# A mixture-of-experts stage with side work: the order of calls on every engine, and side work in fixed steps

## The chip, the cores and the metric

The kernel runs on one core of a Trainium2 chip. The metric is device time in microseconds (us), the median of several runs. Names of engines: PE is TensorE's matmul, PEld its weight load, DVE is VectorE, ACT is ScalarE, POOL is GpSimd, SP is SyncE, which here only issues transfers.

## The reference, cut to what matters

Two blocks of cross attention and feed-forward follow one another on x of shape (4, 512, 512), fp32, so there are 2048 tokens of width 512:

```
x = x + tanh(g) * L0_xattn(layernorm(x), ctx)      # int8 codes, 16 heads
x = x + tanh(g) * L0_ffn(layernorm(x))             # 8 experts, top 2, and a shared expert
x = x + tanh(g) * L1_xattn(layernorm(x), ctx)      # fp8 codes, self and cross attention
x = x + tanh(g) * L1_ffn(x)                        # ternary weights
```

The second line is the mixture of experts. A token goes to two experts; each expert computes `silu(x w1) * (x w3) @ w2` with 448 hidden units. The fourth line's weights are made ternary: each of its two weight matrices is scaled by the mean of its absolute values, rounded and limited to -1, 0 and 1. That mean and these codes do not depend on x.

## The kernel before

**The stages.** `xattn_int8` is the first line, `moe` the second, `attend_and_feed` the third and fourth. Nearly the whole kernel is bound by TensorE. While the mixture of experts runs, the kernel also prepares weights for what follows. There are two kinds of this side work:

- *Split pieces.* `split_weights` makes 80 steps (class `Split`). Each loads a piece of 128 x 512 fp32 (`s_raw`, 256 KB), on VectorE scales and centres it (`centre`; pieces of the projection have nothing to centre), casts it to a high part on ScalarE and subtracts for the low part on GpSimd (`cut`, `s_hl`), and stores both parts (512 KB). The pool has two buffers each for `s_raw` and `s_hl`.
- *Block 4.* `Ffn.weights` makes a list of 26 steps for the ternary weights: 12 sums of absolute values of 128 x 1408 pieces (704 KB each, line 2287), two steps that turn sums into a scale (from line 2295), and 12 codings (the piece loaded again, three VectorE instructions, lines 2310 to 2312, and a store of 176 KB at 2313). They use four buffers in turn (`t_raw`).

**The mixture of experts.** Tokens are sorted by expert into 39 slots of 128 rows through `slots_in`, by indirect transfers. Before the slots, a written-out plan (`Beat`) runs the shared expert: `m_up` products and then 16 `m_po` products, and with them scales and scatters the rows of the slots and prepares 23 split pieces. The plan's last tick is 40; the last split piece is loaded in tick 36, cut in tick 38 and stored in tick 39.

Then comes the loop over slots. TensorE's order in slot s is: the up products of slot s+1 (`up`, 16 weight loads and matmuls into `pu` and `pw`), the transposes of slot s's hidden units (`turn_hidden`) and of slot s+2's rows (`turn_in`), and the down products of slot s-1 (`down`, into `po`). Each matmul in the program is two in the profile. SyncE loads the expert's w13 (two halves, line 1204) for slot s+3, into the buffer that `up(s+1)` gives back, and its w2 (line 1226) for slot s+1. There are two buffers of each, and a load is skipped where the slot two before had the same expert; the owner of the slot is read into registers first (`load`, line 1197). ScalarE issues the loads of rows (1208) and the stores of the results (1267).

**What sets the order.** Each engine runs its instructions in the order in which they stand in its queue. A wrapper, `Ordered`, makes the framework keep the order of the calls on one engine. Calls that don't go through it are placed by the framework's own scheduler, which may put them ahead of calls that stand before them in the text. In the slots of the kernel before only TensorE's calls go through `Ordered`; those of the other engines, the split pieces and block 4's steps do not. Line 245 is the wrapper's line, so every ordered instruction has L245 in the profile, and evacuations by `k.evac`, which takes VectorE and ScalarE in turn, have L110 and L112.

The last part of a slot's body, before:

```
            for _ in range(-(-len(split) // max(1, SLOTS - 5 - s))):
                split.pop(0)(ps)
            if ternary:
                ternary.pop(0)()
```

With 57 pieces left this is two a slot in slots 0 to 22 and one in slots 23 to 33. `split.pop(0)(ps)` loads, centres, cuts and stores in one call.

Of the kernel before, what the change touches and what calls it, by code (L numbers as in the profile page):

```python
# [11 lines left out]
F32 = mybir.dt.float32  # L12
# [5 lines left out]
AF = mybir.ActivationFunctionType  # L18
ALU = mybir.AluOpType
# [889 lines left out]
def moe(k, split, codes8, router, scratch, ffn):  # L909
# [13 lines left out]
    with ExitStack() as ctx:  # L923
# [270 lines left out]
        def load(s):  # L1194


            e = got["e", s] = nc.values_load(
                owners[:, s : s + 1], engines=(mybir.EngineType.SP,), min_val=0, max_val=E - 1,
                skip_runtime_bounds_check_because="it is at most E - 1 by construction",
            )  # L1200
            got["new", s] = None if s < 2 else e != got["e", s - 2]
            for c in (0, KC // 2):
                some = slice(c, c + KC // 2)
                nc.sync.dma_start(w13[s % 2][:, some], a["w13"][e][:, some], cond=got["new", s])

        def load_rows(s):
            work = p6.tile([P, 4, D], F32, tag="m_big", name=f"m_work{s}")
            rows = nc.scalar.dma_start(work[:, 0, :], rows_in[ts(s, P), :])
            for scatter in scatters:
                tc.add_manual_dep(  # L1210
                    rows.ins, scatter.name,
                    mybir.DependencyInfo(mybir.DependencyClass.Sync, mybir.DependencyReason.DATA),
                    reason="any of them may write a row of the slot",
                )

            tc.add_manual_dep(
                rows.ins, silus[-1].name,
                mybir.DependencyInfo(
                    mybir.DependencyClass.NoSync, mybir.DependencyReason.SCHED_ONLY
                ),  # L1220
                reason="order of ScalarE's queue",
            )
            got["work", s] = work

        def load_down(s):
            nc.sync.dma_start(w2[s % 2], a["w2"][got["e", s]], cond=got["new", s])

        PE = Ordered(tc, nc.tensor)

        def turn_in(s):  # L1230
            work = got["work", s]
            pt = ps_m.tile([P, KC, P], F32, tag="ps_m")
            for c in range(KC):
                PE.transpose(pt[:, c, :], work[:, 0, ts(c, P)], k.ident)
            k.evac(work[:, 1, :].rearrange("p (c t) -> p c t", c=KC), pt)

        def up(s):
            work, w = got["work", s], w13[s % 2]
            pu = ps_h.tile([P, HID], F32, tag="ps_h")
            pw = ps_h.tile([P, HID], F32, tag="ps_h")  # L1240
            for c in range(KC):
                for half, pp in enumerate((pu, pw)):
                    PE.matmul(
                        pp, lhsT=work[:, 1, ts(c, P)], rhs=w[:, c, half, :],
                        start=(c == 0), stop=(c == KC - 1),
                    )
            nc.scalar.activation(work[:, 2, 0:HID], pu, AF.Silu)
            nc.vector.tensor_tensor(work[:, 2, 0:HID], work[:, 2, 0:HID], pw, ALU.mult)  # L1248

        def turn_hidden(s):  # L1250
            work = got["work", s]
            pt = ps_m.tile([P, NHC, P], F32, tag="ps_m")
            for m in range(NHC):
                PE.transpose(pt[:HC, m, :], work[:, 2, ts(m, HC)], k.ident)
            k.evac(work[:HC, 3, :].rearrange("p (c t) -> p c t", c=NHC), pt[:HC])

        def down(s):
            work, w = got.pop(("work", s)), w2[s % 2]
            po = ps_o.tile([P, D], F32, tag="ps_o")
            for m in range(NHC):  # L1260
                PE.matmul(
                    po, lhsT=work[:HC, 3, ts(m, P)], rhs=w[:, m, :],
                    start=(m == 0), stop=(m == NHC - 1),
                )
            y = p4.tile([P, D], F32, tag="m_row", name=f"m_y{s}")
            nc.scalar.activation(y, po, AF.Copy, scale=k.tg[:, 2:3])
            nc.scalar.dma_start(rows_out[ts(s, P), :], y)

        ctxT, ws = [], {}

# [7 lines left out]
                ctxT[b], a["ctxT"][:, ts(b, S)].rearrange("(c p) t -> p c t", p=P)  # L1278
            )

        ternary = ffn.weights(codes8, ps_o)
        for s in range(4):
            load_rows(s)
        for s in range(2):
# [3 lines left out]
        up(0)  # L1288
        load(2)
        turn_in(1)  # L1290
        for s in range(SLOTS):

            if s + 1 < SLOTS:
                up(s + 1)
            if s + 3 < SLOTS:
                load(s + 3)
            turn_hidden(s)
            if s + 2 < SLOTS:
                turn_in(s + 2)
            if s:  # L1300
                down(s - 1)
                if s + 1 < SLOTS:
                    load_down(s + 1)
            if s + 4 < SLOTS:
                load_rows(s + 4)
            for _ in range(-(-len(split) // max(1, SLOTS - 5 - s))):
                split.pop(0)(ps)
            if ternary:
                ternary.pop(0)()
            if s == SLOTS - 4:  # L1310
                load_weights(0)
                load_context(0)
            elif s == SLOTS - 2:
                for c in range(KC):
                    centred(k, ws[0][:, c, 0:256], 2, nc.vector)
# [181 lines left out]
def split_weights(k):  # L1497
# [15 lines left out]
    class Split:  # L1513
# [23 lines left out]

        def store(self, SY):
            SY.dma_start(self.to, self.hl.bitcast(F32))

        def __call__(self, pool):
            self.load(pool, nc.sync)
            self.centre(nc.vector)
            self.cut(nc.scalar, nc.gpsimd)
            self.store(nc.sync)

    steps = []
    for i in range(NP):
# [680 lines left out]
class Ffn:  # L2229
# [32 lines left out]
        nc.sync.dma_start(self.mid[b * TB + t], k.x[:, t, :])  # L2262
        nc.sync.dma_start(k.x[:, t, :], self.mid[(b + 1) * TB + t])

    def weights(self, codes8, psum):


        k, nc, a = self.k, self.k.nc, self.k.a
        of = []
        for name, n, cols in (("w_gu", KC, 2 * F), ("w_dn", NF, D)):  # L2270
            flat = a[name].rearrange("p n o -> p (n o)")
            of.append((name, [flat[:, ts(i, F)] for i in range(n * cols // F)]))
        turn, got = [0], {}

        def piece(src):
            w = codes8.pool.tile(
                [P, 2048], F32, tag=f"g_xq{turn[0] % 4}", name=f"t_raw{turn[0]}"
            )
            turn[0] += 1
            nc.sync.dma_start(w[:, 0:F], src)  # L2280
            return w

        def add(name, i, n, src):
            if i == 0:
                got["part", name] = k.const.tile([P, n], F32, name=f"part_{name}")
            w = piece(src)
            nc.vector.tensor_reduce(
                got["part", name][:, i : i + 1], w[:, 0:F], AX.X, ALU.add,
                apply_absolute_value=True,
            )  # L2290

        def scale(name, n, inv):
            part = got["part", name]
            tot = k.small.tile([P, 1], F32, tag="t_tot")
            nc.vector.tensor_reduce(tot, part, AX.X, ALU.add)
            pm = psum.tile([P, 1], F32, tag="ps_o", name="t_pm")
            nc.tensor.matmul(pm, lhsT=k.ones, rhs=tot, start=True, stop=True)
            mean = k.small.tile([P, 1], F32, tag="t_mean")
            nc.vector.tensor_scalar(mean, pm, 1.0 / (P * n * F), 1e-5, ALU.mult, ALU.max)
            got["sc", name] = sc = k.const.tile([P, 1], F32, name=f"sc_{name}")  # L2300
            nc.vector.reciprocal(sc, mean)
            nc.vector.reciprocal(inv, sc)
            if name == "w_dn":
                nc.vector.tensor_tensor(inv, inv, k.tg[:, 3:4], ALU.mult)

        def code(name, src, lo):
            w = piece(src)
            sc = got["sc", name]
            raw, c8 = w[:, 0:F], w[:, F : F + F // 4].bitcast(F8)
            nc.vector.tensor_scalar(raw, raw, sc, 1.0, ALU.mult, ALU.min)  # L2310
            nc.vector.tensor_scalar(raw, raw, -1.0, MAGIC, ALU.max, ALU.add)
            nc.vector.tensor_scalar(c8, raw, -MAGIC, None, ALU.add, saturate=False)
            nc.sync.dma_start(self.codes[:, lo : lo + F], c8)

        steps, lo = [], 0
        for name, pieces in of:
            steps += [partial(add, name, i, len(pieces), p) for i, p in enumerate(pieces)]
        for (name, pieces), inv in zip(of, (self.inv_g, self.inv_dg)):
            steps.append(partial(scale, name, len(pieces), inv))
        for name, pieces in of:  # L2320
            for p in pieces:
                steps.append(partial(code, name, p, lo))
                lo += F
        return steps

# [98 lines left out]
```

## Time and profile before

| | |
|---|---|
| median of 3 runs | 3391.55 us (3390.26 to 3392.24) |
| profiled execution, its own time | 3394.43 us |
| its span | 3392.6 us |
| mean granted clock of TensorE | 0.985 |
| busy in the span: PE, DVE, ACT, POOL | 95%, 63%, 46%, 41% |
| the shared expert's products, `m_up` and `m_po` | 491 to 690 us |
| the slots, first `pu` to last `po` | 694 to 1138 us |
| issues of w13 halves and w2 | 117, of which most are skipped |

Times inside the profile are counted from the span's start. A line of a timeline gives the start, the duration, the engine, the line of the kernel, the operation, output<-input, and in brackets how long the engine sat idle before it and what ended that. A line of the waits gives who waited for whom, the total in us, the number of times and the longest.

### The profile page before, as it was taken

What the parts mean: (1) busy time and instruction counts of PE and PEld (TensorE: products, weight loads), DVE (VectorE), ACT (ScalarE), POOL (GpSimd) and SP (SyncE); (2) the same over time, 40 slices, a digit from 0 to 9 for tenths busy, and PEclk for the clock granted to TensorE, in tenths of its full rate; (3) what the DMA queues carried; (4) which work ended last, traced back from release to release, by engine and by line L of the source; (5) the groups of instructions that cost most, each with busy time, mean ns of one, the idle gap of its engine ahead of it and who ended that gap; (6) DMA issues with size and microseconds to landing.
All of it is one profiled execution on the core that took longest, in us unless ns stands there. A gap on an engine that the chain in (4) does not pass through costs nothing.

```text
span 3392.6 us, 47675 instructions
## 1 busy us (share of the span) xinstructions
PE 3218.7 (95%) x15466; PEld 2141.9 (63%) x15488; DVE 2144.5 (63%) x4551; ACT 1572.0 (46%) x4524; POOL 1377.5 (41%) x1568
## 2 busy tenths in 40 slices
PE   7999899899889999899999999999999999999997
PEld 4555554345445444577777777767777767777775
DVE  6888886443262455355587676687666786766567
ACT  4676661122222233455554555545545545555543
POOL 2001013412221255244466544566544575545443
PEclk9999999999899999999999999999999999999998
DMA  5544325845765444522232423323333322333210
GB/s 164 156 123 122 75 71 176 308 157 183 256 229 196 171 149 156 171 99 94 100 112 81 135 97 121 100 87 112 116 112 103 103 100 95 108 118 106 90 67 23
DMA packets 222008, 436.15 MB, mean 129 GB/s; under 512 B 23616, under 2 KB 82496, under 8 KB 220096
## 3 DMA queue, kind: packets, MB, share of 16 engines
q1 hardware_dynamic: 205408, 395.87, 35.6%
q10 hardware_dynamic: 11232, 20.45, 1.8%
q0 software_dynamic: 5120, 16.78, 1.5%
q8 instruction: 125, 2.05, 0.2%
q14 instruction: 123, 1.01, 0.1%
HBM read 387.33 MB, written 100.20 MB: 144 GB/s over the span
## 4 chain that ended last, share of the span: by engine, by line
PE 48%; DVE 8%; POOL 1%; ACT 1%; issue 1%; DVEq 0%; POOLq 0%; ACTq 0%
PE ps_w L245 11%; PE pss L245 10%; PE ps_p L245 10%; PE ps_o L245 9%; PE ps_t L245 8%; DVE f_y L245 2%; DVE nm L245 1%; DVE t_work L245 1%; DVE g_hn L245 1%; DVE f_e L245 1%; DVE g_pT L245 1%; POOL g_rstd L245 1%; DVE t_sm L245 1%; ACT junk L245 0%; DVE f_c L245 0%
## 5 line engine op out<-in xcount | busy, mean ns | idle before, releaser
L245 DVE TENSOR_REDUCE nm<-pss 128x1 f32<-128x512 f32 x768 | 523.6, 685 | 120.8 <-PE pss L245 116.2
L245 PEld LDWEIGHTS ps_w<-g_pT,g_v 128*128 128x128 f32 x2048 | 387.5, 190 | 299.5 <-issue 223.7
L245 ACT ACTIVATE g_p<-pss,nm 128x512 f32<-128x512 f32 x512 | 350.6, 685 | 479.3 <-DVE nm L245 439.2
L245 PE MATMUL ps_w<-g_pT,g_v 128*128 128x256 f32 x2048 | 528.5, 381 | 24.3 <-DVE f_y L245 13.6
L245 PE MATMUL pss<-g_kT,g_qT 128*128 128x512 f32 x1024 | 524.1, 594 | 0.9 <-ACT g_p L245 0.9
L245 POOL TENSOR_SCALAR g_p<-g_p,rs 128x512 f32<-128x512 f32 x512 | 366.8, 717 | 382.3 <-DVE rs L245 373.9
L245 PE MATMUL ps_t<-ident,g_p 128*128 128x128 f32 x2048 | 307.5, 273 | 0.0
L245 POOL TENSOR_TENSOR g_rstd<-ss,neghalf 128x4 f32<-128x4 f32 (+1 forms) x192 | 184.9, 963 | 298.5 <-ACT ss L245 298.5
L245 PE MATMUL ps_p<-g_wq,g_xq 128*128 128x512 f32 x1024 | 281.5, 416 | 5.6 <-DMA g_wq<-s_q 5.1
L245 PE MATMUL ps_o<-g_wp,g_cq 128*128 128x512 f32 x1024 | 286.1, 422 | 0.0
L245 DVE COPY g_pT<-ps_t 128x512 f32<-128x512 f32 x244 | 167.0, 684 | 166.6 <-PE ps_t L245 166.2
L245 POOL TENSOR_TENSOR f_t<-f_y,f_c 128x512 f32<-128x512 bf16 (+1 forms) x180 | 206.2, 1146 | 155.0 <-DVE f_c L245 87.2
L245 ACT COPY g_pT<-ps_t 128x512 f32<-128x512 f32 x268 | 155.9, 582 | 232.6 <-PE ps_t L245 232.6
L245 PEld LDWEIGHTS ps_t<-ident,g_p 128*128 128x128 f32 x2048 | 243.7, 141 | 26.3 <-POOL g_p L245 1.1
L245 ACT ACTIVATE p<-pss,nm 128x512 f32<-128x512 f32 x256 | 177.2, 693 | 134.0 <-DVE nm L245 127.8
L245 PE MATMUL m_pk<-m_wx,m_ctxT 128*128 128x512 f32 x512 | 230.0, 592 | 0.0
L245 PEld LDWEIGHTS ps_o<-g_wp,g_cq 128*128 128x128 f32 x1024 | 196.2, 192 | 41.3
L245 PEld LDWEIGHTS ps_p<-g_wq,g_xq 128*128 128x128 f32 x1024 | 190.9, 190 | 49.2 <-issue 6.8
L1536 POOL TENSOR_TENSOR s_hl<-s_raw,s_hl 128x512 fp32r<-128x512 f32 x57 | 76.4, 1350 | 341.8 <-ACT s_hl L1535 320.7
L245 DVE RECIPROCAL rs<-g_sm 128x1 f32<-128x1 f32 x512 | 82.5, 161 | 202.2 <-ACT g_p L245 200.3
L245 ACT ACTIVATE junk<-ps_p 128x128 f32<-128x128 f32 x640 | 176.7, 276 | 67.1 <-PE ps_p L245 52.9
L1248 DVE TENSOR_TENSOR m_work<-m_work,pw 128x448 f32<-128x448 f32 x39 | 24.2, 620 | 256.9 <-PE pw L245 220.5
(339 smaller groups left out, 5913.1 us busy)
## 6 DMA issues: line engine op xcount, KB each, us to landing
m_w<-in_w_dram SPq DMA_DIRECT2D x117, 896.0 KB
g_wp<-s_proj SPq DMA_DIRECT2D x128, 512.0 KB
g_wq<-s_q SPq DMA_DIRECT2D x128, 256.0 KB
g_wq<-s_qx SPq DMA_DIRECT2D x128, 256.0 KB
st_k<-hl_k SPq DMA_DIRECT2D x128, 128.0 KB
st_q<-hl_q SPq DMA_DIRECT2D x128, 128.0 KB
s_proj<-s_hl SPq DMA_DIRECT2D x32, 512.0 KB
s_kx<-m_ring SPq DMA_DIRECT2D x64, 256.0 KB
```

Source lines behind the costliest of these rows:

```text
L245: return lambda *args, **kw: self.tc.keep_in_program_order(call(*args, **kw))
L1248: nc.vector.tensor_tensor(work[:, 2, 0:HID], work[:, 2, 0:HID], pw, ALU.mult)
L1536: GE.tensor_tensor(hl[:, 1, :], self.raw, hl[:, 0, :].bitcast(F32), ALU.subtract)
```

## The change

All calls of the slots go through `Ordered`, so VectorE, ScalarE, GpSimd and SyncE keep the order of the text, as TensorE did: the loads of rows and of expert weights, the evacuations (rows now always on VectorE, hidden units always on ScalarE), the activations and the stores.

The split pieces are shared out evenly over 34 slots (one or two in each) and their calls are spread over three slots: a piece of slot s is loaded at the end of slot s-1, centred and cut in slot s, and stored at the beginning of slot s+1.

Block 4's list has 27 steps, each in two parts: `send` loads the piece, and the rest works on it. A step works in slot s = 0 to 26, and the piece is sent for two slots ahead. The two totals of the sums are a step of their own (12), ahead of the two scales (13, 14); codings follow in 15 to 26.

```
-                nc.sync.dma_start(w13[s % 2][:, some], a["w13"][e][:, some], cond=got["new", s])
+                SY.dma_start(w13[s % 2][:, some], a["w13"][e][:, some], cond=got["new", s])
...
-            rows = nc.scalar.dma_start(work[:, 0, :], rows_in[ts(s, P), :])
+            rows = AE.dma_start(work[:, 0, :], rows_in[ts(s, P), :])
...
-            nc.sync.dma_start(w2[s % 2], a["w2"][got["e", s]], cond=got["new", s])
-
-        PE = Ordered(tc, nc.tensor)
+            SY.dma_start(w2[s % 2], a["w2"][got["e", s]], cond=got["new", s])
...
-            k.evac(work[:, 1, :].rearrange("p (c t) -> p c t", c=KC), pt)
+            VE.tensor_copy(work[:, 1, :].rearrange("p (c t) -> p c t", c=KC), pt)
...
-            nc.scalar.activation(work[:, 2, 0:HID], pu, AF.Silu)
-            nc.vector.tensor_tensor(work[:, 2, 0:HID], work[:, 2, 0:HID], pw, ALU.mult)
+            AE.activation(work[:, 2, 0:HID], pu, AF.Silu)
+            VE.tensor_tensor(work[:, 2, 0:HID], work[:, 2, 0:HID], pw, ALU.mult)
...
-            k.evac(work[:HC, 3, :].rearrange("p (c t) -> p c t", c=NHC), pt[:HC])
+            AE.copy(work[:HC, 3, :].rearrange("p (c t) -> p c t", c=NHC), pt[:HC])
...
-            nc.scalar.activation(y, po, AF.Copy, scale=k.tg[:, 2:3])
-            nc.scalar.dma_start(rows_out[ts(s, P), :], y)
+            AE.activation(y, po, AF.Copy, scale=k.tg[:, 2:3])
+            AE.dma_start(rows_out[ts(s, P), :], y)
...
-        ternary = ffn.weights(codes8, ps_o)
+        ternary = ffn.weights(codes8, ps_o, (VE, PE, SY))
+
+
+        n, over = len(split), SLOTS - 5
+        pieces = [
+            [split.pop(0) for _ in range((s + 1) * n // over - s * n // over)] for s in range(over)
+        ] + [[]] * 6
...
         turn_in(1)
+        for piece in pieces[0]:
+            piece.load(ps, SY)
+        for send, _ in ternary[:2]:
+            send()
         for s in range(SLOTS):
+            for piece in pieces[s - 1] if s else ():
+                piece.store(SY)
...
-            for _ in range(-(-len(split) // max(1, SLOTS - 5 - s))):
-                split.pop(0)(ps)
-            if ternary:
-                ternary.pop(0)()
+            for piece in pieces[s]:
+                piece.centre(VE)
+                piece.cut(AE, GE)
+            for piece in pieces[s + 1]:
+                piece.load(ps, SY)
+            if s < len(ternary):
+                ternary[s][1]()
+            if s + 2 < len(ternary):
+                ternary[s + 2][0]()
```

In `Ffn.weights` the calls go to the ordered engines, and each step becomes a pair:

```
+        def step(src, work, *args):
+            n, here = len(steps), []
+
+            def send():
+                if src is not None:
+                    w = codes8.pool.tile(
+                        [P, 2048], F32, tag=f"g_xq{n % 4}", name=f"t_raw{n}"
+                    )
+                    SY.dma_start(w[:, 0:F], src)
+                    here.append(w)
+
+            steps.append((send, lambda: work(*here, *args)))
...
+        def total():
+            for name, _ in of:
+                got["tot", name] = k.small.tile([P, 1], F32, tag="t_tot", name=f"t_tot_{name}")
+                VE.tensor_reduce(got["tot", name], got["part", name], AX.X, ALU.add)
```

More of the change, by code (lines that the diff above doesn't have):

```diff
@@ L1539, in store @@
             SY.dma_start(self.to, self.hl.bitcast(F32))
[L1541 to L1545, printed above, removed]
     steps = []
@@ L2263, in change, with weights @@
         nc.sync.dma_start(k.x[:, t, :], self.mid[(b + 1) * TB + t])
-    def weights(self, codes8, psum):
-        k, nc, a = self.k, self.k.nc, self.k.a
+    def weights(self, codes8, psum, engines):
+        k, a = self.k, self.k.a
+        VE, PE, SY = engines
         of = []
@@ L2272, in weights, with add @@
             of.append((name, [flat[:, ts(i, F)] for i in range(n * cols // F)]))
[L2273 to L2283, printed above, removed]
+        steps, got = [], {}
+        def step(src, work, *args):
[8 more added lines that the diff above has]
+            steps.append((send, lambda: work(*here, *args)))
+        def add(w, name, i, n):
             if i == 0:
                 got["part", name] = k.const.tile([P, n], F32, name=f"part_{name}")
-            w = piece(src)
-            nc.vector.tensor_reduce(
+            VE.tensor_reduce(
                 got["part", name][:, i : i + 1], w[:, 0:F], AX.X, ALU.add,
@@ L2290, in add @@
             )
+        def total():
+            for name, _ in of:
+                got["tot", name] = k.small.tile([P, 1], F32, tag="t_tot", name=f"t_tot_{name}")
+                VE.tensor_reduce(got["tot", name], got["part", name], AX.X, ALU.add)
         def scale(name, n, inv):
-            part = got["part", name]
-            tot = k.small.tile([P, 1], F32, tag="t_tot")
-            nc.vector.tensor_reduce(tot, part, AX.X, ALU.add)
             pm = psum.tile([P, 1], F32, tag="ps_o", name="t_pm")
-            nc.tensor.matmul(pm, lhsT=k.ones, rhs=tot, start=True, stop=True)
+            PE.matmul(pm, lhsT=k.ones, rhs=got["tot", name], start=True, stop=True)
@@ L2298, in scale @@
             mean = k.small.tile([P, 1], F32, tag="t_mean")
-            nc.vector.tensor_scalar(mean, pm, 1.0 / (P * n * F), 1e-5, ALU.mult, ALU.max)
+            VE.tensor_scalar(mean, pm, 1.0 / (P * n * F), 1e-5, ALU.mult, ALU.max)
             got["sc", name] = sc = k.const.tile([P, 1], F32, name=f"sc_{name}")
-            nc.vector.reciprocal(sc, mean)
-            nc.vector.reciprocal(inv, sc)
+            VE.reciprocal(sc, mean)
+            VE.reciprocal(inv, sc)
             if name == "w_dn":
-                nc.vector.tensor_tensor(inv, inv, k.tg[:, 3:4], ALU.mult)
@@ L2306, in code @@
-        def code(name, src, lo):
-            w = piece(src)
+                VE.tensor_tensor(inv, inv, k.tg[:, 3:4], ALU.mult)
+        def code(w, name, lo):
             sc = got["sc", name]
             raw, c8 = w[:, 0:F], w[:, F : F + F // 4].bitcast(F8)
[L2310 to L2313, printed above, removed]
@@ L2315, in weights @@
-        steps, lo = [], 0
+            VE.tensor_scalar(raw, raw, sc, 1.0, ALU.mult, ALU.min)
+            VE.tensor_scalar(raw, raw, -1.0, MAGIC, ALU.max, ALU.add)
+            VE.tensor_scalar(c8, raw, -MAGIC, None, ALU.add, saturate=False)
+            SY.dma_start(self.codes[:, lo : lo + F], c8)
+        lo = 0
         for name, pieces in of:
-            steps += [partial(add, name, i, len(pieces), p) for i, p in enumerate(pieces)]
+            for i, p in enumerate(pieces):
+                step(p, add, name, i, len(pieces))
@@ L2318, in weights @@
+        step(None, total)
         for (name, pieces), inv in zip(of, (self.inv_g, self.inv_dg)):
-            steps.append(partial(scale, name, len(pieces), inv))
+            step(None, scale, name, len(pieces), inv)
         for name, pieces in of:
             for p in pieces:
-                steps.append(partial(code, name, p, lo))
+                step(p, code, name, lo)
                 lo += F
```

## The prediction

> **What bounds the kernel now.** I read the page, then the table by stage, then the waits, then the timeline of the longest stall. TensorE is the bound: 3218.7 of 3392.6 us busy, and the granted clock falls below full only after it has stood idle. So only stalls of TensorE can be won. By stages (columns: stretch, us, busy us of PE, PEld, DVE, ACT, POOL, granted clock, DMA share, GB/s):
>
> ```profile
> 529.00:617.00 88.00, 86.92 (x205) 35.67 (x205) 56.72 (x110) 10.46 (x19) 40.69 (x36) 1.00 0.71 245
> 617.00:690.00 73.00, 60.64 (x133) 25.41 (x132) 32.38 (x57) 10.47 (x18) 22.36 (x19) 0.95 0.87 297
> 690.00:711.00 21.00, 16.14 (x49) 8.38 (x47) 7.78 (x16) 3.64 (x7) 3.79 (x3) 0.92 0.53 175
> 711.00:846.00 135.00, 134.79 (x421) 70.25 (x421) 44.77 (x86) 34.11 (x59) 26.64 (x20) 1.00 0.48 165
> 846.00:932.00 86.00, 69.73 (x195) 34.95 (x195) 23.96 (x55) 18.87 (x33) 17.20 (x14) 0.90 0.75 251
> 932.00:1018.00 86.00, 76.73 (x226) 38.91 (x225) 54.18 (x81) 19.76 (x34) 17.88 (x13) 0.94 0.66 231
> 1018.00:1138.00 120.00, 120.00 (x369) 61.85 (x368) 24.04 (x44) 25.85 (x44) 12.13 (x10) 1.00 0.55 191
> ```
>
> The slots run from 694 to 1138. From 711 to 846 and after 1018 TensorE is full and one slot takes 10.32 us (first `pu` to first `pu`). In between I summed each slot's excess over 10.32 us: slots 13 to 19 24.6 us (slot 15 alone 9.45), slots 22 to 26 13.7 us. That is 38.3 us, half-clock time included. The shared expert's second product (617 to 690) has 17 us too much: 16 tiles of eight matmuls at 0.43 us are 55 us, and they take 72.
>
> The waits of PE and of SyncE's queue in the slots (total us, times, longest):
>
> ```profile
> PE pu L245 <- DMA m_w<-in_w_dram: 18.8, 4, 9.2
> PE po L245 <- DMA m_w<-in_w_dram: 6.9, 5, 2.8
> ...
> SPq L1539 <- POOL s_hl L1536: 220.3, 55, 10.4
> ```
>
> The longest stall in the timelines of SP's queue and of PE:
>
> ```profile
> 855.17 1.56 SPq L1539 DMA_DIRECT2D s_qx<-s_hl  x2
> 856.82 0.41 SPq L1523 DMA_DIRECT2D s_raw<-in_w_qx_dram  x1
> 857.33 0.66 SPq L1523 DMA_DIRECT2D s_raw<-in_w_kv_dram  x1
> 859.64 1.12 SPq L1204 DMA_DIRECT2D m_w<-in_w_dram  x2
> ...
> 865.64 1.83 PE L245 MATMUL pu<-m_w,m_work 128*128 128x448 f32 x2 [9.20 <-DMA m_w<-in_w_dram]
> ```
>
> TensorE waits for expert weights, and these were not slow but late. SP issued nothing from 845.3 to 855.2: it stood at the store of a split piece (L1539), whose POOL subtraction waited for VectorE, which worked off two codings of block 4 (L2310 to L2312, 837 to 853) first. The weights went out at 859.6 and 860.4 and both halves (1.84 MB) had landed by 865.5, in 5.9 us. Where SP skips a load (same expert, 0.09 us instead of 0.34), TensorE waits for the skipped issue all the same (946.3, 998.0).
>
> In the stage ahead, VectorE's and TensorE's timeline:
>
> ```profile
> 628.48 0.74 DVE L245 SCALAR_TENSOR_TENSOR x_res<-m_po,tg,x_res 128x512 f32<-128x512 f32 x1
> 636.79 1.62 DVE L2287 TENSOR_REDUCE part_w_gu<-t_raw 128x1 f32<-128x1408 f32 x1 [7.57 <-DMA t_raw<-in_w_gu_dram]
> 638.33 0.74 DVE L245 SCALAR_TENSOR_TENSOR x_res<-m_po,tg,x_res 128x512 f32<-128x512 f32 x1
> ...
> 639.12 5.40 PE L245 MATMUL m_po<-m_w,m_h 112*128 112x512 f32 x8 [4.44 <-DVE x_res L245]
> ```
>
> All 12 sums of block 4 run here (537 to 650), a stage earlier than the code puts them. VectorE stands 7.6 us for a piece issued at 628.1, and the residual add behind it frees PSUM too late.
>
> **The change, part by part.** *1. The 12 sums and four code loads leave 533 to 674.* This takes 12 x 1.62 = 19.4 us off VectorE and 16 x 0.72 = 11.5 MB off the transfers. The two stalls that end at a sum (4.71 and 4.44 us) and their two half-clock windows (3.4 us each, so 1.7 us lost each) go: 12.5 us. Late in the stage 2.3 and 0.6 us remain, which are centrings waiting for their own pieces. I take -12; bounds -6 (the split pieces become the next late thing) to -17 (all of it).
>
> *2. The first slots' loads lose their early place.* Before, the first expert's w13 went out at 535, w2 at 651, the second w13 at 659 and 667, four rows at 627, all among the earlier stage's instructions. In call order they stand behind that stage's last store on SP (691.5, 1.4 us after its last matmul, E = 690.1) and behind its last cut on ACT (689.5). Four rows, a store and w13, w2, w13 are 6.2 MB; at the 297 to 313 GB/s of the rows above that is some 20 us, so the second `up` ends near E+24 and the third begins at E+25 to E+26. Before it began at 710.7, E+20.6, with 3.5 us of idle and a half-clock window in it. +5; bounds 0 (larger transfers run faster) to +9.
>
> *3. Slots 13 to 19.* SP now meets, in each slot: stores of the last slot's pieces (cut already, so no wait), the two w13 halves of slot s+3 (3.1 and 6.2 us into the slot, as TensorE releases the buffer), w2, the next pieces' loads (they wait for this slot's cuts, 13.7 and 15.0 us by the chain: down ends 10.4, scaling 0.69, two issues 0.33, cast 0.62, POOL 1.27 each), then block 4's store and load. w13 is out 14 us ahead of its use instead of zero, and w2 17 us ahead. The late issue ends. What is late next is the transfers themselves. A slot with two pieces, rows and a block 4 piece moves 1.57 + 0.52 + 0.72 MB; slots 13, 14, 15 add 1.84 MB of w13 each, 15 to 17 add 0.92 MB of w2 each, and the codes store 0.18. Slots 13 to 17 sum to 21.3 MB: 72 us at 297 GB/s, 62 at 341 (297 over its share 0.87), against 51.6 us of TensorE. So 11 to 20 us too much, of which rows and expert weights can be late by about 5; with half-clock time I leave 12 of the 24.6: -12, bounds -20 to 0.
>
> *4. Slots 20 to 26.* 2.74 MB a slot is 265 GB/s, under 297. VectorE has 0.62 + 0.68 + two centrings of 2.04 + a coding of 2.7 (0.93 + 0.88 + 0.88) to 5.8 (1.96 each), 8 to 11 us of 10.3; 8 of the 13 pieces of slots 15 to 22 are of the projection and have no centring. I leave 4 of 13.7: -10, bounds -13.7 to +5.
>
> *5. Slots 0 to 12.* They gain a sum and 0.72 MB each: 165 GB/s become about 250. Hidden as long as a piece lands in time: where VectorE waited, this took 2.7 to 5.5 us, and the new order leaves 4.3 before VectorE is ready, and 3 us more before the gate of the next slot. If that cover is gone, each late us costs one. +2; bounds 0 to +12.
>
> Swapping the evacuations (turned rows to VectorE, 0.68 us; turned hidden to ACT, 0.58) costs nothing: both have 3.4 us of down's matmuls above them. The split `total` step is two reduces of 0.15 us. VectorE's gate and copy are now queued behind the last slot's centring and coding, ACT's Silu behind its casts; the next slot's transposes wait for that copy. That is the price in the rivals.
>
> [...]
>
> **Sum.** -12 + 5 - 12 - 10 + 2 = -27 us. The profiled execution took 3394.4 us (span 3392.6), 2.9 above the median of the three runs, 3391.55; 3391.6 - 27 = 3364.
>
> **Rivals.** *A: transfers take the place of the late issue.* The stalls of slots 13 to 26 stay at about 38 us, now waiting for transfers issued in time; only parts 1 and 2 count: 3391.6 - 12 + 5 = 3384. For it: 251 GB/s and share 0.75 from 846 to 932 already. Against: the stalls there follow late issues.
>
> *B: slower, by the ring of two buffers.* `s_raw` and `s_hl` have two each, and a piece now passes cast and subtraction 1.9, issue and landing 4.7, centring 2.05, sum 1.6 (coding 2.7 to 4.8) ahead of SP's store, 1.3 of issues, and the landing of 1.77 MB, 7.5: 19.1 us with a sum, 20.2 to 22.3 with a coding, in two slots of 20.6. If pieces land in 9.5 us instead of 4.3, as the block 4 piece did at 628 (8.7), a slot with a sum grows by 1.8 us, one with a coding by 3.4: 12 x 5.2 = 62 us in place of 38. With parts 1 and 2, 3391.6 - 7 - 38 + 62 = 3408. It decides from 8.6 us on. Against: no centring that VectorE waited for in the slots came later than 5.5.
>
> *C: the change doesn't order what matters.* The owner's read ahead of each w13 is not called through the ordered queue; were SP still to reach w13 behind late work, everything but part 1 and 2 stays and part 2 may cost its 9: 3389.
>
> **Numbers.** Forecast 0.66, A 0.12, B 0.14, C 0.08. About 0.2% (6.8 us) is what a measurement can tell from no change: faster below 3384.8, slower above 3398.4. The forecast is faster but for its tail, A lies on the line (0.08 to 0.04), C is mostly same; 0.73, 0.11, 0.16. The likeliest case's own range is 3346 to 3382; the range to hold the time 8 in 10 reaches over A and C: 3344 to 3392.
>
> **What would show it.** Right: no L2287 before the slots; m_po's 16 tiles in under 62 us; the third `pu` 24 to 27 us after the last m_po; w13 issued at each slot's third and sixth us; SP's waits for POOL harmless; slots 20 to 26 near 10.3 us. Wrong: PE waiting for `m_work` copies of VectorE in sum slots (B), or slots 13 to 26 as long as now though the weights go out early (A).

## The result, and the profile after

The changed kernel takes 3366.5 us (median; 3361.9 to 3372.2), against 3391.9 (3390.3 to 3392.6) for the kernel before, run beside it: ratio 0.9927, 95% interval 0.9909 to 0.9944. It is faster by 25 us; 27 were forecast. The profiled execution took 3367.0 us, span 3365.2.

Four stretches by stage (columns as before: stretch, us, busy of PE, PEld, DVE, ACT, POOL, granted clock, DMA share, GB/s):

```profile
616.00:671.00 55.00, 55.00 (x129) 24.07 (x127) 23.45 (x43) 8.66 (x14) 16.45 (x13) 1.00 0.68 239
671.00:694.00 23.00, 17.72 (x50) 9.26 (x50) 4.37 (x7) 1.67 (x3) 1.26 (x1) 0.85 0.57 191
842.00:897.00 55.00, 45.84 (x133) 23.06 (x132) 25.08 (x48) 10.80 (x20) 9.15 (x7) 0.94 0.92 311
897.00:990.00 93.00, 85.31 (x256) 42.85 (x254) 42.73 (x62) 20.43 (x37) 16.08 (x13) 0.98 0.68 230
```

The shared expert's second product fills its 55 us without a gap, at full clock; before it took 72.4. The transition to the slots (671 to 694) is no better than it was: 17.7 of 23 us busy at a clock of 0.85, before 16.1 of 21 at 0.92. Two stretches of slots still lose. In 842 to 897 the transfers are busy to 0.92 at 311 GB/s, so that they can be the limit there; the share alone does not show it (e10_late_only, below, has 0.93 in the same stretch and hardly loses). In 897 to 990 they are at 0.68 and 230, and are not.

To place every microsecond, I read each run's trace in the prediction's way: the last `m_po`'s end E, the third `pu` counted from E, and each slot's excess over 10.32 us. These add up to the end of the slots: of before to after, 18.9 - 1.8 + 0 - 4.0 + 11.5 + 2.1 = 26.7 us, and the last `po` begins at 1137.6 and 1110.8. The experiments are in the same table:

| | E | third `pu` | slots 10–12 lose | 13–19 | 20–28 | 29–37 | last `po` begins |
|---|---|---|---|---|---|---|---|
| before | 689.9 | E+20.8 | 0.0 | 24.6 | 13.7 | 0.0 | 1137.6 |
| after | 671.0 | E+22.6 | 4.0 | 13.1 | 11.6 | 0.0 | 1110.8 |
| e3_b4_free | 684.7 | E+22.5 | 0.0 | 14.2 | 35.3 | 0.0 | 1145.2 |
| e4_b4_only | 672.0 | E+22.3 | 0.0 | 30.7 | 23.7 | 2.4 | 1147.3 |
| e6_rows_free | 669.5 | E+17.1 | 4.2 | 15.0 | 12.5 | 0.0 | 1106.8 |
| e1_hl3 | 669.8 | E+18.3 | 0.5 | 12.6 | 8.1 | 0.0 | 1097.8 |
| e2_store_first | 671.2 | E+21.7 | 0.0 | 13.1 | 4.3 | 0.1 | 1099.0 |
| e5_no_t_raw | 670.0 | E+23.1 | 2.1 | 7.8 | 0.0 | 0.0 | 1091.5 |
| e7_hl3_store_first | 671.1 | E+20.1 | 0.0 | 13.8 | 4.3 | 1.8 | 1099.6 |
| e10_late_only | 672.9 | E+22.6 | 3.9 | 1.6 | 8.5 | 15.3 | 1113.1 |
| e8_codes_late | 671.0 | E+17.4 | 0.0 | 3.5 | 5.0 | 4.3 | 1089.6 |
| e11_late_rows_store | 670.2 | E+17.2 | 0.0 | 3.1 | 5.4 | 5.1 | 1089.5 |
| e9_late_rows_hl3 | 669.1 | E+17.1 | 0.0 | 2.9 | 5.0 | 3.5 | 1086.0 |

(Slots 2 to 9 lose 0.1 in all of them but e4_b4_only, where it is 7.8.) Each row is one profiled execution, and the repeated times of one kernel lie up to 10 us apart. Rows whose slots have the same calls differ by up to 2 us in a column (after and e6_rows_free), so differences of that size carry no weight. The profiled executions of e8_codes_late and e9_late_rows_hl3 were 7 and 6 us under their kernels' medians: these two rows flatter.

The waits in the slots of after (who for whom, total us, times, longest; the last is of SP's queue):

```profile
DVE m_work L245 <- ACT m_work L245: 85.3, 15, 10.9
ACT s_hl L245 <- DMA s_proj<-s_hl: 62.1, 13, 9.8
...
PE pu L245 <- DVE m_work L245: 16.3, 7, 5.9
...
PE pu L245 <- DMA m_w<-in_w_dram: 3.3, 2, 1.8
```

```profile
SPq L245 <- DMA slots_out<-m_y: 127.6, 25, 8.9
SPq L245 <- POOL s_hl L245: 60.9, 29, 5.1
```

The wait of `pu` for expert weights fell from 18.8 to 3.3 us, and SP's for GpSimd from 220.3 to 60.9. SP now stands longest for something new: for the landing of a slot's results, which ScalarE stores (`slots_out`). In slots 20 to 28 some of these waits are those of a piece's store whose transfer, by the trace's semaphores, is counted on the same semaphore as the results' store before it; it went out only when that had landed (at 913.21, after 5.4 us; the results' store, issued at 907.89, had landed at 913.19). No run takes this wait away. On TensorE's side stands a chain that the waits of before hardly had: `pu` waits for a copy on VectorE, VectorE for ScalarE, ScalarE for the landing of a store (`s_proj<-s_hl`, 62 us, and the other targets of `s_hl`, 48 more). The timeline of one such slot, ScalarE's, then SP's queue, then VectorE's and TensorE's:

```profile
927.95 0.62 ACT L245 CAST s_hl<-s_raw 128x512 fp32r<-128x512 f32 x1 [9.76 <-DMA s_proj<-s_hl]
929.14 0.62 ACT L245 CAST s_hl<-s_raw 128x512 fp32r<-128x512 f32 x1 [0.57 <-DMA s_proj<-s_hl]
929.66 0.54 ACT L245 ACTIVATE m_work<-pu 128x448 f32<-128x448 f32 x1
```

```profile
915.47 2.80 SPq L245 DMA_DIRECT2D s_raw<-in_w_proj_dram  x2
918.36 0.38 SPq L245 DMA_DIRECT2D ffn_codes<-t_raw  x1
918.80 0.42 SPq L245 DMA_DIRECT2D t_raw<-in_w_gu_dram  x1
919.27 2.83 SPq L245 DMA_DIRECT2D s_proj<-s_hl  x2
```

```profile
930.23 0.62 DVE L245 TENSOR_TENSOR m_work<-m_work,pw 128x448 f32<-128x448 f32 x1 [9.27 <-ACT m_work L245]
930.77 0.68 DVE L245 COPY m_work<-pt 128x512 f32<-128x512 f32 x1
...
931.51 1.02 PE L245 MATMUL pu<-m_w,m_work 128*128 128x448 f32 x2 [2.62 <-DVE m_work L245]
```

Two pieces had been cut in the slot before. The first was done by 910.86, but its store goes out at 919.27, behind the next loads, the codes' store and block 4's load. By the trace's semaphores it lands 8.6 us later, at 927.85, and only then can ScalarE cast into that one of the two `s_hl`; the second store (issued at 921.78) lands at 929.07, and frees the other. The Silu (`ACTIVATE m_work<-pu`), whose `pu` TensorE had finished with the transposes' start at 924.42, stands behind both casts because the order of calls puts it there; gate, copy and the next `pu` follow in turn, and TensorE has stood idle for 2.6 us.

In slots 13 to 19 TensorE's longest idle time comes through VectorE's order instead, VectorE's line first:

```profile
874.48 0.62 DVE L245 TENSOR_SCALAR s_raw<-s_raw,pcol_sb 128x256 f32<-128x256 f32 x2 [8.86 <-DMA s_raw<-in_w_kv_dram]
...
883.46 1.12 PE L245 MATMUL pu<-m_w,m_work 128*128 128x448 f32 x1 [5.86 <-DVE m_work L245]
```

VectorE stood until a late piece had landed, then centred two pieces and did a whole coding (878.53 to 882.28), and only behind these the gate and the copy that `pu` waited for.

### The profile page after: what moved, and what is told of

Read it like the earlier page. It is cut to its first block, busy times and chain, and to the rows that moved or that the text cites. A ratio compares the mean times of both kernels' runs of the same rounds, so it can differ in the third digit from the quotient of the medians.

```text
span 3365.2 us, 47699 instructions
## 1 busy us (share of the span) xinstructions
PE 3215.0 (96%) x15488; PEld 2141.2 (64%) x15488; DVE 2140.2 (64%) x4551; ACT 1570.8 (47%) x4524; POOL 1376.1 (41%) x1568
## 4 chain that ended last, share of the span: by engine, by line
PE 74%; DVE 13%; DMA 5%; ACT 2%; issue 2%; POOL 2%; SPq 1%; DVEq 0%; ACTq 0%; POOLq 0%
PE pss L245 11%; PE ps_w L245 11%; PE ps_p L245 10%; PE ps_o L245 9%; PE ps_t L245 8%; PE m_pk L245 7%; PE po L245 4%; PE pu L245 3%; PE pw L245 3%; PE pt L245 2%; DVE nm L245 2%; PE m_up L245 2%; DVE f_y L245 2%; DMA s_proj<-s_hl 1%; PE pv L245 1%
## 5 line engine op out<-in xcount | busy, mean ns | idle before, releaser
L245 PE MATMUL ps_w<-g_pT,g_v 128*128 128x256 f32 x2048 | 530.2, 382 | 23.9 <-DVE f_y L245 13.8
L245 POOL TENSOR_TENSOR s_hl<-s_raw,s_hl 128x512 fp32r<-128x512 f32 x80 | 102.7, 1291 | 363.3 <-ACT s_hl L245 331.3
L245 PEld LDWEIGHTS pt<-ident,p 128*128 128x128 f32 x1024 | 117.7, 141 | 90.7 <-issue 41.6
```

What stands on the lines that cost most here:

```text
L245: return lambda *args, **kw: self.tc.keep_in_program_order(call(*args, **kw))
```

## The experiments

**One part at a time.** First the rest of the change with block 4 as before, then block 4 alone.

```
e3_b4_free, against after (in short); weights() as before, outside the wrapper
-            if s < len(ternary):
-                ternary[s][1]()
-            if s + 2 < len(ternary):
-                ternary[s + 2][0]()
+            if ternary:
+                ternary.pop(0)()

e4_b4_only, against before: the reverse; weights() as in the change
```

> The changed kernel with block 4's steps as in the kernel before (one call a slot, left to the scheduler), all else as changed. If the sums' place is what delayed the shared expert's second product, its 16 tiles take about 72 us again instead of 55 and the third pu starts some 17 us later, near 710; slots 10 and 11 lose nothing; about 3378 us. If the gain of that stage came from something else (the rows' or the weights' loads), the 16 tiles stay near 55 us, and the time is at most 3366.

> The kernel before, with block 4's part of the change alone: its sums and codes one step a slot in the order of calls, sent for two slots ahead; expert weights, rows, split pieces and evacuations as before. If the parts stand each by itself (the stage ahead is freed by the sums leaving it, the slots by the order of the rest): the 16 m_po tiles in about 55 us in place of 72, E some 18 us earlier than before, slots 13 to 19 still losing about 24 us and 20 to 28 about 14: 3373 us. Rival, by the run in which the rest of the change without block 4's steps lost 35 us in slots 20 to 28: the parts need each other, and ordered steps of block 4 between unordered split pieces cost the slots over 50 us in all, which takes back most of the 18: 3385 to 3392.

Measured: 3402.6 us for the first, ratio to before 1.0033 (1.0020 to 1.0045), and 3405.3 for the second, 1.0034 (1.0021 to 1.0047). Each half alone is slower than before; together they are 25 us faster. For the first, 3378 or at most 3366 had been expected, so both readings missed the time. The gains of the steps do not add up from parts. In e3_b4_free the sums slide back ahead of the slots (E only 5 us earlier), and slots 20 to 28 lose 35 us. SP's queue, otherwise in order, stands at the store of codes (L2318) with all the rest behind it (its waits for GpSimd are longer, 105.2 us), and TensorE waits for VectorE's copies twice as long as in after; the first line is of SP's queue, the second of PE. How the one leads to the other I did not follow slot by slot:

```profile
SPq L2318 <- DVE t_raw L2317: 36.9, 8, 5.9
...
PE pu L245 <- DVE m_work L245: 32.4, 10, 7.1
```

In e4_b4_only the first part's gain is there in full (E = 672.0, 16 tiles in 55.7 us) and the slots give back more than all of it. SP still stands at each split piece's store as before the change, with w2 behind it, and the ordered matmul of block 4's scale (`t_pm`) holds TensorE once, because the totals it needs had slid behind unordered split pieces on VectorE. PE's waits, then SP's:

```profile
PE po L245 <- DMA m_w<-in_w_dram: 26.6, 12, 4.6
PE t_pm L245 <- DVE t_tot_w_dn L245: 18.8, 1, 18.8
```

```profile
SPq L1544 <- POOL s_hl L1541: 234.7, 56, 9.0
```

For this run I had put the gains' sum (3373) ahead of the rival (3385 to 3392); it came out beyond the rival.

**The rows of the first slots.**

```
-rows = AE.dma_start(work[:, 0, :], rows_in[ts(s, P), :])
+rows = (AE if s > 3 else nc.scalar).dma_start(work[:, 0, :], rows_in[ts(s, P), :])
```

> The changed kernel, but the rows of the first four slots are sent for as before, outside the order of ACT's queue. If these rows are what part 2 of the change costs: they go out at about 627 again, TensorE's 2.6 us of idle ahead of slot 0's transposes (673.6) goes, and the third pu begins at E + 20 in place of E + 22.6: about 3364 us, 2.5 less than the changed kernel's 3366.5. Rival: the expert weights behind them are late anyway (w2 of slot 1 and the third w13); slot 0 starts earlier and the third pu stays at E + 22 to 23: 3366 to 3367.

Measured: 3360.2 us (0.9896, 0.9880 to 0.9913), 6 less than the change, and the third `pu` at E+17.1 instead of E+22.6. The wait itself was 2.6 us, so it was worth twice its length. TensorE and granted clock show why; after, then this run:

```profile
673.62 0.78 PE L245 MATMUL pt<-ident,m_work 128*128 128x128 f32 x4 [2.58 <-DMA m_work<-slots_in]
675.28 1.83 PE L245 MATMUL pu<-m_w,m_work 128*128 128x448 f32 x2 [0.88 <-DVE m_work L245]
```

```profile
675.00:681.00 6.00, 5.72 (x8) 2.82 (x9) 0.13 (x1) 0.00 (x0) 0.00 (x0) 0.51 0.79 264
```

```profile
671.00:677.00 6.00, 6.00 (x16) 3.04 (x17) 0.00 (x0) 0.48 (x1) 0.00 (x0) 1.00 0.81 240
```

After the idle time TensorE ran 6 us at a granted clock of 0.51, with 8 matmuls in place of 16. The first `up` took 8.85 us instead of 6.09 (its first `pu` to the next transposes): 2.6 + 2.8 = 5.4 of the 5.5 us. In after the rows wait behind the last split piece's cast (670.35 to 670.97, and the four issues right behind it), which is where the wrapper's order puts them.

**The ring of `s_hl`.** Three buffers instead of two; then the store in the slot of its cut, ahead of the next loads; then both. To make room for the third buffer, short-lived tables of the router share a place with a w13 buffer (the edits are shown in short).

```
e1_hl3                                              e2_store_first
+wide = ...tc.tile_pool(name="m_hl", bufs=3)        -    for piece in pieces[s - 1] if s else ():
-self.hl = hl = self.pool.tile([P, 2, 512], ...)    -        piece.store(SY)
+self.hl = hl = self.wide.tile([P, 2, 512], ...)         ...  piece.cut(AE, GE)
                                                    +    for piece in pieces[s]:
                                                    +        piece.store(SY)
                                                         for piece in pieces[s + 1]:  # loads
```

> The changed kernel with three buffers for the cut pieces (s_hl) instead of two; room for the third by letting short-lived router tiles share the place of the first expert's weights. Theory 1, ring: the casts of slots 10, 11 and 20 to 28 wait until the store two pieces earlier has landed, and ScalarE's Silu, VectorE's gate and the copy of the next rows stand behind the cast. Then slots 20 to 28 lose under 4 us instead of 11.6, slots 10 and 11 under 1 instead of 4.0, and the time is about 3354 us. Theory 2, transfers: the same volume still has to move, the slots lose what they lost, and the time stays near 3366. In slots 14 to 19 (13.1 us lost, 311 GB/s) both expect little: at most 4 us less.

> The changed kernel with each piece stored in the slot of its cut, ahead of the next pieces' loads and of block 4's store and load on SP's queue, instead of at the beginning of the next slot. Buffers as they are. Theory 1, ring: the store goes out about 1 to 3 us earlier and no 0.72 MB load stands ahead of it, so it lands 3 to 5 us earlier; slots 20 to 28 lose under 4 us instead of 11.6, and the time is 3353 to 3358 us. Theory 2, transfers: order alone moves nothing, 3366. A third way: the next pieces' loads, now behind the store, come late, VectorE waits for them, and the slots lose more than now: above 3370.

> The changed kernel with both cures of the ring: three s_hl buffers, and a piece's store issued in the slot of its cut, ahead of the next loads. If the two cures act on different waits (the buffer for the cast, SP's queue for the store): slots 20 to 28 lose under 2 us (8.1 with the buffers alone, 4.3 with the store alone), 10 to 12 nothing, 13 to 19 still 12 to 13, the third pu at E + 18: 3346 to 3349 us. If both shorten the same wait, from a cut to the landing of its store, they do not add: 20 to 28 lose about 4 us and the time is 3351 to 3353.

Measured: 3352.7 us (0.9882, 0.9866 to 0.9899), 3358.3 (0.9904, 0.9887 to 0.9920) and both together 3354.9 (0.9881, 0.9865 to 0.9898). Either cure takes slots 10 to 12 to nothing or nearly (0.0 and 0.5) and cuts slots 20 to 28, from 11.6 to 8.1 and to 4.3; both together give 4.3 again. So they act on one and the same wait, from a cut to the landing of its store. In slots 20 to 28 a store went out 4.3 us after its subtraction's end on average in after (9.7 at most) and landed 6.1 us after that; in e2_store_first it is 1.2 and 3.3. In e1_hl3 it is 8.2 and 4.0, and the third buffer covers it only in part: under 4 us had been expected in these slots, and 8.1 remain. Its time came out as expected because it also won in the transition, which was luck: its last cast ahead of the slots happened to fall at 668.1, so the rows left 2.5 us earlier and the clock stayed full (third `pu` at E+18.3). Slots 13 to 19 keep their 13 us in all three.

**The transfers.** First without block 4's second loads: the codings work on pieces that the sums had loaded, so 8.65 MB are not moved (the edits are shown in short).

```
e5_no_t_raw                                   e10_late_only
-if src is not None:                           step(None, scale, name, len(pieces), inv)
+if n > 14:                                   +for _ in range(5):
+    here.append(got["kept", n % 4])          +    step(None, int)
+elif src is not None: ...                     # codings in slots 20 to 31, not 15 to 26
```

> The changed kernel without the second load of block 4's pieces: the 12 codings work on the last pieces that were summed (the codes are those of other data). This leaves out 8.65 MB of transfers in slots 13 to 24 and nothing else. Transfers as the bound of slots 14 to 19: their loss falls from 13.1 us to under 5, and SP's order as the bound would leave it at 13. For slots 20 to 28 both theories expect less: transfers 0 to 2 us, the ring 3 to 6, because the cut pieces' stores no longer stand behind a load. Time 3344 to 3354 us.

Measured: 3349.1 us (0.9876, 0.9860 to 0.9892). Slots 13 to 19 lose 7.8 instead of 13.1 (under 5 had been expected), and 20 to 28 nothing. By what was put on record, nothing lost there speaks for transfers, and 3 to 6 us for the ring. But order alone, with every byte still moved, takes these slots to 4.3 (e2_store_first), and here the stores went out 2.2 us after the subtraction and landed 4.3 us later: with fewer loads on the way the same ring holds. Ring and transfers act together. Of the 7.8 us, more than half is one idle time of 4.5 us, for VectorE's copy behind a late piece and a coding (`pu` at 876.10). Then the same loads, moved away from the expert weights of slots 13 to 19, with both cures of the ring and without:

> As the run with both cures, and the twelve codings five slots later: slots 20 to 31 in place of 15 to 26, so that their loads and stores (0.72 and 0.18 MB each) do not meet the expert weights of slots 13 to 19. If transfers are what slots 13 to 19 still lose: 12 to 13 us there become about 8 (7.8 in the run without block 4's loads), slots 20 to 31 lose 1 to 3 us, and the time is 4 to 5 us under that of both cures without this: 3343 to 3346 us. Rival: slots 13 to 19 are bound by the expert weights' own place in the queue and keep 12 us; then nothing is won, and the codings that now share slots 27 to 31 with centrings cost up to 3 us: 3348 to 3354.

> The changed kernel with one edit: the twelve codings five slots later (slots 20 to 31 in place of 15 to 26). If slots 13 to 19 lose their 13 us to transfers, of which block 4's loads are the part that need not be there: 13 to 19 lose about 4 us (3.5 in the run that also had both cures of the ring), third pu and slots 10 to 12 as in the changed kernel (E + 22.6 and 4 us), and the ring's loss moves with the codings: 20 to 31 lose 12 to 14 us: 3357 to 3360 us. Rival, the cures of the ring were what freed slots 13 to 19 there: they keep 10 us or more and the time is 3364 to 3367.

Measured: 3353.3 us (0.9882, 0.9865 to 0.9898) with the cures, 3368.7 (0.9925, 0.9911 to 0.9938) without. In both, slots 13 to 19 are nearly free (3.5 and 1.6 us), so what they lost was block 4's codings meeting the expert weights: 10 to 12 us. The loads alone were 5 of these; the rest goes with the codings' other parts there (three VectorE instructions ahead of the gate, the codes' store, the places of both in the queues), which no run separates. That the transfers' share is no proof of a limit shows here: in 842 to 897 e10_late_only has 0.93 and 299 GB/s, and TensorE is busy for 54.1 of 55 us. Without the cures the ring takes it all back: slots 20 to 37 lose 23.8 us, where 12 to 14 had been expected, and ScalarE waits for the landing of `s_proj` stores as before (56.5 us in 14 waits, 62.1 in 13 in after).

By its times e8_codes_late is not shown to be faster than e7_hl3_store_first (3346 to 3357 against 3352 to 3358; 3343 to 3346 had been expected); its slots 13 to 19 lose less in the one trace.

**The version that these point to.** Stores first, codings late, first rows out of ACT's order, with two and with three `s_hl`:

> The changed kernel with three edits: stores ahead of the next loads, codings five slots later, first rows outside ACT's order; s_hl keeps its two buffers. If the buffers add nothing where the store goes out early (4.3 us lost in slots 20 to 28 with it and without the third buffer, 4.3 with both): third pu at E + 17, 13 to 19 lose 3 to 5 us, 20 to 31 5 to 9: 3345 to 3350 us. Rival, two buffers with twelve codings beside the centrings of slots 20 to 31 are too few: over 10 us there and 3352 or more.

> As the run before it, with three s_hl buffers. Third pu at E + 17, 10 to 12 nothing, 13 to 19 lose 3 to 5 us, 20 to 28 5 and 29 to 37 up to 4: 3343 to 3347 us; if the third buffer is worth nothing beside the early store, the same as the run before it within 2 us. Rival: the rows of the first slots were already early in the run with the late codings (third pu at E + 17.4), so that the time stays at its 3353 (3346 to 3357).

Measured: 3347.4 us both (0.9863, 0.9848 to 0.9878; 0.9864, 0.9849 to 0.9879). That is 19 us under the change (3366.5, ratio 0.9927), with three edits of a few lines each; the third buffer adds nothing that can be seen. With two buffers, in e11_late_rows_store, the two stretches that still lost in after read:

```profile
842.00:897.00 55.00, 52.91 (x163) 27.06 (x162) 17.05 (x36) 14.12 (x26) 11.34 (x9) 1.00 0.83 286
897.00:990.00 93.00, 88.31 (x266) 45.12 (x265) 59.31 (x87) 23.67 (x40) 17.57 (x14) 0.98 0.74 245
```

Its table of waits no longer lists ScalarE waiting for a store of `s_hl`; `pu` waits 7.6 us for VectorE's copies, from 16.3 in after. Some 14 us are left in slots 13 to 37, where codings now share slots with centrings. I did not go after them.

## Why the prediction came out, step by step

The number was right within 3 us by luck: the stage ahead gave 7 us more than forecast and slots 20 to 28 gave 8 less, and the first slots' loads (3 better) and slots 0 to 12 (2 worse) cancel too.

1. *The sums leave the stage ahead: right in kind, mis-sized.* Forecast -12, with -17 as the bound "all of it"; measured -18.9 on E (tiles 72.4 to 55.1 us, and a start 1.6 us earlier; the trace of before has E at 689.9, the prediction 690.1). The two half-clock windows that part 1 counted are in the trace of before, with granted clocks of 0.51 (629.4 to 632.8) and 0.52 (639.6 to 643.1); in after the whole second product ran at 1.00. The step that failed is "late in the stage 2.3 and 0.6 us remain": those waits had been for pieces that stood behind the sums' loads and work, and they went too (in e4_b4_only as well, 55.7 us).
2. *The first slots' loads: +1.8 for a forecast of +5, and for another reason.* Two things I had not seen cancel within it. SP's loads did not lose their early place: the first w2 and the second w13 still went out among the split pieces (634.5; 641.9 and 649.6), as they had before. That the owner's register reads ahead of them, which are not called through the wrapper, break its chain would explain it; that is the mechanism of rival C, here as a help, but no run tests it. What did move behind the last cast were the four rows, worth 5.5 us by e6_rows_free, about half of it time at a granted clock of 0.51. I had priced the step as transfer time, which it was not. The step's bound of 0 took larger transfers to run faster; in the trace of before, after 1018, loads of 256 KB (`s_raw` of the projection) landed a median of 3.75 us after their issue, and loads of 896 KB (w13 halves and w2) 6.16 us.
3. *Slots 13 to 19: right in number, half in mechanism.* Forecast -12, measured -11.5. The weights go out early and the late issue is gone, as said. Of transfers as the next limit, 5 of the 13 us left are shown: they go with block 4's second loads (e5_no_t_raw). That the rest of the codings costs as much again in these slots was not in the sum, and the longest idle time of TensorE there (5.9 us) is a wait for VectorE's copy, behind a late piece's centring and a coding: the price that the prediction had left to its rivals.
4. *Slots 20 to 28: wrong.* Forecast -10, measured -2.1. I summed VectorE's work per slot and the transfers' rate, both with room, and both have it (42.7 of 93 us busy; 230 GB/s). The step that failed is the one that took these for the only limits; the ring of two `s_hl`, through stores issued 4.3 us late and landing 6.1 us after issue on average, is what holds the slots, and I had it only as rival B, on the condition that pieces land late (from 8.6 us on). That condition did not hold: the pieces landed 2.5 to 3.5 us after their issue in these slots, and the stores were late. The steady 1.8 us of each sum slot and 3.4 of each coding slot, by which B was priced, did not come. Here the order itself carries the wait to TensorE: the Silu stands behind the cast. ScalarE's rows show it: the Silu began at 929.66, behind the second cast (at 929.14), though TensorE had finished its `pu` by 924.42.
5. *Slots 0 to 12: +4.0 for +2*, within 0 to 12: the same ring, in slots 10 and 11. It ends with either cure.

Part 4 of the forecast gave a coding 2.7 to 5.8 us. In the trace of before, the coding's second instruction (L2311) took 0.88 us when no GpSimd subtraction (1.27 us) ran beside it, and 1.84 to 1.96 when one did; why, no run shows. In after such meetings were rare: 2 of the 36 coding instructions took over 1.3 us (1.84 and 1.91), against 13 before; the 36 add up to 34.8 us, from 45.0. In e8_codes_late, where the ring is cured, 10 of the 36 took over 1.3 us again (42.8 in all).

Rival A (3384) is true in part: transfers did take the place of the late issue in slots 13 to 19, but with at most 13 us, not 38. Rival B (3408) named the right ring at too high a price, and its sign (`pu` waiting for VectorE's copies) did appear, 16.3 us in 7 waits.

## What to carry to other kernels

Giving every engine the order of the text removed the late issues here (`pu` waited 3.3 us for expert weights, from 18.8), but made each wait a wait of everything behind it (the Silu at 929.66, behind two casts that waited for landings): for each ordered queue, ask which instruction waits for a landing, and what TensorE needs from behind it. A store that frees a buffer belongs ahead of the loads that only fill one (with that edit alone slots 20 to 28 lost 4.3 us, from 11.6). And parts of such a change must be tried together: each of the two halves here was slower alone, and the late codings alone won nothing (ratio 0.9925 against 0.9927), because the ring took back what slots 13 to 19 gave. Beside the cures their gain is seen in slots 13 to 19 of the traces, not in the times.

## What the runs showed of the hardware that was not expected

Nearly equal idle times were followed by different clocks. With 1.18 us before the first slot's transposes and 0.88 after them (e1_hl3), TensorE went on at full clock; with 1.20 and 0.88 (e7_hl3_store_first) it did not: in the 6 us after, the granted clocks were 1.00, with 16 matmuls, and 0.72, with 12. The second:

```profile
673.80:679.80 6.00, 5.93 (x12) 2.85 (x13) 0.00 (x0) 0.00 (x0) 0.00 (x0) 0.72 0.84 291
```

What decides between the two no run shows; each is one profiled execution.

A store of 512 KB took 2.6 to 10.9 us from issue to landing in the slots of after, by the trace's semaphores, while loads ran beside it.
